# The fourth quarter of each middle head's exponentials goes through a transposing DMA, and values and the feed-forward halves change places

## The chip, the cores and the metric

One core of a Trainium2 chip runs the whole program in one launch. The metric is device time in microseconds: how long the one execution takes on the chip. The engines named below are TensorE (PE; its weight loads are listed as PEld), VectorE (DVE), ScalarE (ACT), GpSimd (POOL) and SyncE (SP), which here issues most of the DMAs.

## The reference

The program computes two layers on x (4 batches of 512 rows of 512). The first layer (a state space mixer and a mixture of experts) is not touched by the change. The second is cross-attention with 16 heads of 128 on a context of 512 rows, followed by a feed-forward block with ternary weights and 8-bit rows:

```python
    def _L1_xattn_ref(hidden_states, encoder_hidden_states, Wq, Wk, Wv, Wo, gq, gk):
        ...
        scale = 1.0 / np.sqrt(D)
        q = (hidden_states @ Wq).reshape(B, Sq, H, D)
        k = (encoder_hidden_states @ Wk).reshape(B, Skv, H, D)
        v = (encoder_hidden_states @ Wv).reshape(B, Skv, H, D)
        q = rmsnorm(q, gq)
        k = rmsnorm(k, gk)
        scores = jnp.einsum('bqhd,bkhd->bhqk', q, k) * scale
        attn = jax.nn.softmax(scores, axis=-1)
        out = jnp.einsum('bhqk,bkhd->bqhd', attn, v)
        out = out.reshape(B, Sq, H * D)
        return out @ Wo
    ...
        def bitlinear(x, w):
            xq = x + jax.lax.stop_gradient(activation_quant(x) - x)
            wq = w + jax.lax.stop_gradient(weight_quant(w) - w)
            return jnp.einsum('bsi,oi->bso', xq, wq)
        h = bitlinear(x, w1)
        h = jax.nn.gelu(h, approximate=False)
        return bitlinear(h, w2)
    ...
    x = x + _L1_xattn_ref(_layernorm(x, axis=-1), ctx_1024, ...)
    x = x + _L1_ffn_ref(_layernorm(x, axis=-1), L1_ffn_w1, L1_ffn_w2)
```

All values are 32-bit floats. What the change touches is the way from the scores to `attn` times `v`: the exponentials have queries on the partitions, and the product with `v` wants the context rows there, so each 128 x 512 block of weights must be transposed.

## The kernel before

The stage in question is the function `attend`. There are 64 heads over the batches, numbered n from 0 to 63 (16 a batch; groups of four heads share a load of `Wq` and `Wo`). Each head has four quarters i of 128 query rows. The main loop runs over units u = 4n + i, and the Python order in which instructions are written is the order in each engine's queue; every engine takes its queue in order.

In unit (n, i) are written, in this order:

- `scores(n, i)`: one PE matmul pair into `psc` (L1987; two such banks), DVE's row maximum `mx` (L1990), ACT's exponential `e` with its row sum (L1993).
- in unit i = 2, `values(n - 1)`: four PE matmuls (L2059, eight records in the trace) of `v` with `eT` of the head before, and ACT's copy of the result to `oT` (L2061). There is one `eT` buffer.
- what `front` holds for this unit: `project` (L2068, i = 0), `queries` (L1953, i = 1; ACT writes the squares `sq`, L1956), `turn_q` (L1980) and `turn_x` (L1907), and the feed-forward work on PE (`ffn_up` L2137, `ffn_hT` L2101, `ffn_down` L2172).
- `weights(n, i - 1)`: DVE divides `e` by its sum (L1998, L1999). Then `split` for that quarter, if it goes by DMA: ACT and POOL each copy one 16-bit half of the 32-bit numbers into `planes` (L2017, L2018; two buffers), and SP issues a transposing DMA from `planes` to `turned` (L2020; three buffers).
- `join` of a quarter whose transpose was issued two units ago: DVE and ACT copy the two halves from `turned` into `eT` (L2027, L2028).
- what `back` holds for this unit: the gathers of the expert rows (`fetch`, POOL L1874) and their sums (`add`, DVE L1882), loads (`load_q` L1917, `load_o` L1925, `load_kv` L1933 to L1939, all on SP), the norm of the queries, `scale_q` (DVE, `qn`, L1971), `split_q` and `join_q` (the same transposing DMA for the queries of three of four blocks), and the row work of the feed-forward block.

Which quarters go by DMA is told by `by_dma`: of heads 4 to 59 the first three; the fourth is transposed on PE by `turn` (four 128 x 128 transposes `pet`, L2052, and ACT's copy from PSUM to `eT`, L2053). In unit i = 1 `turn(n - 1, 3)` stands behind `queries`, and the join of the third quarter ahead of them; values of head n - 1 follow in unit i = 2:

```python
        if i == 2:
            values(n - 1)
        before, landed = divmod(u - 2, KB), divmod(u - 3, KB)
        behind = i == 1 and n < len(heads) - HG
        if not by_dma(*before) and not behind:
            turn(*before)
        if by_dma(*landed) and i == 1:
            join(*landed)
        do(front, u)
```

From batch 1 on, each group of four heads carries the feed-forward block of 128 rows of the batch before. Its up projection is done in two halves (`ffn_up`, with ACT's gelu), its hidden rows are rounded in quarters (`ffn_hq`: DVE, then POOL), transposed in halves (`ffn_hT`: the first on PE with a copy `Th` on ACT, L2102, the second by DMA), and the down projection is done in two halves. All four halves lie in units i = 3.

Of the kernel before, what the change touches and what calls it, by code (L numbers as in the profile page):

```python
# [17 lines left out]
F32 = mybir.dt.float32  # L18
# [3 lines left out]
I16 = mybir.dt.int16  # L22
# [8 lines left out]
P = 128  # L31
# [27 lines left out]
H, HD = 16, 128  # L59
HG = 4  # L60
# [1126 lines left out]
class Keys:  # L1187
# [4 lines left out]
    KB = S // P  # L1192
# [650 lines left out]
def attend(ctx, cm, x_all, w, kv, y_dram, wk, pos, tern, late, ctx_k, wk_k, out):  # L1843
# [6 lines left out]
    pool = {n: ctx.enter_context(tc.tile_pool(name=f"c_p{n}", bufs=n)) for n in (1, 2, 3, 4, 7)}  # L1850
# [6 lines left out]
    KB = S // P  # L1857
# [4 lines left out]
    heads = [(b, g, h) for b, g in groups for h in range(HG)]  # L1862
    xnTs, st = {}, {}
# [101 lines left out]
        nc.gpsimd.tensor_tensor(rq, ms, half, ALU.pow)  # L1965
        st[b, g]["q"] = pq, rq

    def scale_q(b, g):
        pq, rq = st[b, g]["q"]
        qn = st[b, g]["q"] = pool[1].tile([P, HG, HD], F32, name="qn")  # L1970
        nc.vector.tensor_tensor(qn, pq, rq.unsqueeze(2).to_broadcast([P, HG, HD]), ALU.mult)  # L1971

    def turn_q(b, g, i):
# [9 lines left out]
    def scores(n, i):  # L1983

        b, g, h = heads[n]
        pscore = psc.tile([P, S], F32, name="psc")
        nc.tensor.matmul(pscore, st[b, g]["qT"][:, h, i * P:(i + 1) * P], ks[n],  # L1987
                         start=True, stop=True)
        mx = small.tile([P, 1], F32, name="mx")
        nc.vector.tensor_reduce(mx, pscore, AX.X, ALU.max, negate=True)  # L1990
        e = pool[3].tile([P, S], F32, name="e")
        tot = small.tile([P, 1], F32, name="tot")
        nc.scalar.activation(e, pscore, AF.Exp, bias=mx, accum_out=tot)  # L1993
        es[n, i] = e, tot
# [5 lines left out]

    planes, turned = {}, {}

    def by_dma(n, i):
        if not HG <= n < len(heads) - 1:
            return False
        return i < (3 if n < len(heads) - HG else 2)

    def split(n, i):

# [3 lines left out]
    def turn_planes(e):  # L2013

        halves = e.bitcast(I16).rearrange("p (s two) -> p two s", two=2)
        t = pool[2].tile([P, 2, S], I16, name="planes")
        nc.scalar.copy(t[:, 1], halves[:, 1])  # L2017
        nc.gpsimd.tensor_copy(t[:, 0], halves[:, 0])  # L2018
        out = pool[3].tile([P, 2 * KB, P], I16, name="turned")
        nc.sync.dma_start_transpose(out, t.rearrange("p two s -> p (two s)"))  # L2020
        return out

    def join_planes(out, t, i):

        out = out.bitcast(I16).rearrange("p k (s two) -> p two k s", two=2)
        at = slice(i * P, (i + 1) * P)
        nc.vector.tensor_copy(out[:, 1, :, at], t[:, KB:])  # L2027
        nc.scalar.copy(out[:, 0, :, at], t[:, 0:KB])  # L2028

    def join(n, i):  # L2030

        if n not in eTs:
            eTs[n] = pool[1].tile([P, KB, S], F32, name="eT")
        join_planes(eTs[n][:, :, :], turned.pop((n, i)), i)
# [11 lines left out]
    def turn(n, i):  # L2046
        if n not in eTs:
            eTs[n] = pool[1].tile([P, KB, S], F32, name="eT")
        e, _ = es.pop((n, i))
        pt = ptr.tile([P, KB, P], F32, name="pet", tag="pt")  # L2050
        for kc in range(KB):
            nc.tensor.transpose(pt[:, kc, :], e[:, kc * P:(kc + 1) * P], cm.ident)  # L2052
        nc.scalar.copy(eTs[n][:, :, i * P:(i + 1) * P], pt)  # L2053

    def values(n):
        po = pav.tile([HD, S], F32, name="po")
        eT, v = eTs.pop(n), vs.pop(n)
        for kc in range(KB):
            nc.tensor.matmul(po, v[:, kc, :], eT[:, kc, :], start=kc == 0, stop=kc == KB - 1)  # L2059
        oTs[n] = pool[7].tile([HD, S], F32, name="oT")  # L2060
        nc.scalar.copy(oTs[n], po)  # L2061
# [124 lines left out]
    def put(where, u, f, *a):  # L2186
        where.setdefault(u, []).append((f, *a))

    last = len(groups) - 1
    for n, (b, g, h) in enumerate(heads):  # L2190
        j = n // HG
        u = n * KB
        if j < last and j > 0:
            after = groups[j + 1]
            put(front, u + 1, queries, *after, h)
            put(back, u + 2, norm_q, *after)
            put(back, u + 3, scale_q, *after)
            if h < HG - 1:
                put(back, u + 4, split_q, *after, h)
                put(back, u + 6, join_q, *after, h)  # L2200
        if j > 0:
            put(front, u + 4, project, j - 1, h)
        if j < last and j > 0 and h == HG - 1:
            put(front, u + 4, turn_q, *groups[j + 1], h)
        if j > 0:
            put(back, u + 5, take_projected, j - 1, h)
        if j > 0:
            put(back, u, load_q, j + 2, h, h + 1)
            put(back, u + 1, load_o, b, g, h, h + 1)
        put(back, u + 3, load_kv, n + 3)  # L2210
        put(back, u + 3, norm_k, n + 2)
        at = n % H
        if b + 1 < B:
            for k in range(3):
                if 0 <= 3 * (at - 2) + k < NC * TOPK:
                    put(back, u + k, add, 1)
            for k in range(3):
                if 0 <= 3 * (at - 1) + k < NC * TOPK:
                    put(back, u + (0, 1, 3)[k], fetch, 1)
            if at >= 11 and at < 15:  # L2220
                t = (b + 1) * NC + at - 11
                put(back, u + 1, stats, t, "c")
                put(back, u + 3, normed, t, "c")
                put(front, u + 4, turn_x, t)
        if b > 0 and h == 1:
            t = (b - 1) * NC + g
            put(back, u + 1, stats, t, "d")
            put(back, u + 3, ffn_x, t)
            put(back, u + 4, ffn_xq, t)
            put(front, u + 5, ffn_xT, t)  # L2230

            put(front, u + 7, ffn_up, t, 0)
            put(front, u + 11, ffn_up, t, 1)
            for k, at in enumerate((8, 9, 12, 12)):
                put(back, u + at, ffn_max, t, k)
            put(back, u + 12, ffn_h, t)
            for k in range(4):
                put(back, u + 13 + k // 2, ffn_hq, t, k)
            put(front, u + 14, ffn_hT, t, 0)
            put(front, u + 15, ffn_hT, t, 1)  # L2240
            put(front, u + 15, ffn_down, t, 0)
            put(front, u + 19, ffn_down, t, 1)
            put(back, u + 20, ffn_y, t)
            put(back, u + 20, store, t)

    def do(where, u):
        for f, *a in where.pop(u, []):
            f(*a)
# [24 lines left out]
    def later(time, f, *a):  # L2273
        steps.append((time, len(steps), f, a))
# [7 lines left out]
    for n in range(NC * TOPK):  # L2282
        at = n % 16 - KB
        if n >= 16 and 0 <= at < KB:
            at = -1
# [22 lines left out]
    for i in range(NC):  # L2308
        end = START + ((i + 1) * TOPK - 1) * GAP + FLIGHT
        later(end + 0.1, stats, i, "c")  # L2310
        later(end + 2.3, normed, i, "c")
        at = FRONT + i * WINDOW
        later(at, turn_x, i)
        later(at + 0.5, key_task)
        later(at + 2.2, queries, 0, 0, i)
        later(at + 5.6, key_ends)
        later(at + 6.4, norm_q, 0, 0)
        later(at + 6.5, queries, 0, 1, i)
        later(at + 8.5, scale_q, 0, 0)
        later(at + 10, turn_q, 0, 0, i)  # L2320
        later(at + 10.4, key_task)
        later(at + 10.8, norm_q, 0, 1)
        later(at + 12.1, scores, 0, i)
        later(at + 12.9, scale_q, 0, 1)
        later(at + 13, key_ends)
        later(at + 14, turn_q, 0, 1, i)
        if i < KB - 1:
            later(at + 14.7, weights, 0, i)
        if i < KB - 2:
            later(at + 15, turn, 0, i)  # L2330
# [30 lines left out]
    for u in range(KB, len(heads) * KB + 2):  # L2361
        n, i = divmod(u, KB)
        if n < len(heads):
            scores(n, i)
        if i == 2:
            values(n - 1)
        before, landed = divmod(u - 2, KB), divmod(u - 3, KB)
        behind = i == 1 and n < len(heads) - HG
        if not by_dma(*before) and not behind:
            turn(*before)  # L2370
        if by_dma(*landed) and i == 1:
            join(*landed)
        do(front, u)
        if not by_dma(*before) and behind:
            turn(*before)
        if n < len(heads):
            weights(*divmod(u - 1, KB))
            if by_dma(*divmod(u - 1, KB)):
                split(*divmod(u - 1, KB))
        if by_dma(*landed) and i != 1:  # L2380
            join(*landed)
        do(back, u)
        if u == len(heads) * KB:
            weights(*divmod(u - 1, KB))
# [159 lines left out]
```

## Time and profile before

| what | us |
|---|---|
| runs of the kernel before: median (lowest, highest) | 2475.75 (2473.74, 2478.19) |
| the profiled execution's own time | 2472.46 |
| its span | 2470.7 |
| mean granted TensorE clock | 0.979 |
| PE busy in the span | 2337.7 |
| values, L2059: busy, all heads | 236.8 |
| projection of queries, L1953 | 232.7 |
| scores, L1987 | 260.0 |
| output projection, L2068 | 231.2 |

The profile lists one execution. "Busy" is the time in which an engine had an instruction at work; for PE, whose matmuls are pipelined, the ends are modelled. The chain of waits follows the work that ended last back to what released it, so a piece on it is time that the span is made of. In a timeline the bracket behind an instruction tells how long its engine was idle before it, and what ended that. Each float matmul of 128 x 128 by 128 x 512 shows as two records. The attention stage with this loop lies at about 1390 to 2410 us of the span.

### The profile page before, as it was taken

The page shows a single profiled execution, that of the slowest core. Times are in us where ns is not written, and L with a number is a line of the kernel's source. Part 1 is how long each engine was busy: PE and PEld are TensorE (multiplying, and loading weights), DVE is VectorE, ACT ScalarE, POOL GpSimd, SP SyncE. Part 2 cuts the span into 40 slices and gives each one's busy share as a digit, 9 for nine tenths or more (in the row PEclk, how much of TensorE's full clock was granted, in tenths as well). Part 3 has the DMA queues.
Part 4 walks back from the last instruction along what each step waited for, and adds up shares of the span by engine and source line. Part 5 has one row for each costly group of instructions (what it writes and reads, how often), then busy time and mean ns, then how long its engine had stood idle before and what let it go on. Part 6 is the DMA issues. An engine that isn't in the chain of part 4 may idle for free. (4 is left out here: it accounts for less than half of the span.)

```text
span 2470.7 us, 29274 instructions
## 1 busy us (share of the span) xinstructions
PE 2337.7 (95%) x8915; PEld 1275.5 (52%) x8915; DVE 1595.2 (65%) x2848; ACT 1386.1 (56%) x2599; POOL 1344.1 (54%) x1323
## 2 busy tenths in 40 slices
PE   6989998988899999999998999999999999999998
PEld 2555555655556666666674444444444444444443
DVE  6999998966343444444324577667776777666655
ACT  6777777755333333342323466666666767667654
POOL 7999999950344455444434356356544665333323
PEclk8999999998999999999998999999999999999999
DMA  5252626343677777989866568778866887666530
GB/s 212 90 210 95 219 85 232 112 151 119 194 233 227 229 243 236 314 308 336 302 210 211 163 179 217 163 181 187 207 159 149 200 202 173 138 156 147 136 75 24
DMA packets 454245, 458.69 MB, mean 186 GB/s; under 512 B 289239, under 2 KB 330279, under 8 KB 449984
## 3 DMA queue, kind: packets, MB, share of 16 engines
q1 hardware_dynamic: 410622, 299.80, 43.4%
q0 software_dynamic: 41408, 156.76, 19.8%
q8 instruction: 73, 1.20, 0.2%
q14 instruction: 92, 0.75, 0.1%
q10 hardware_dynamic: 2050, 0.18, 0.1%
HBM read 312.74 MB, written 79.82 MB: 159 GB/s over the span
## 5 line engine op out<-in xcount | busy, mean ns | idle before, releaser
L1336 PE MATMUL pg<-xT,wg 128*128 128x284 f32 (+12 forms) x1536 | 392.7, 399 | 2.0 <-ACT xT L1303 1.1
L1990 DVE TENSOR_REDUCE mx<-psc 128x1 f32<-128x512 f32 x256 | 176.1, 688 | 244.4 <-PE psc L1987 244.0
L2018 POOL COPY planes<-e 128x512 int16<-128x512 int16 x174 | 119.1, 684 | 392.3 <-DVE e L1999 230.7
L1336 PEld LDWEIGHTS pg<-xT,wg 128*128 128x128 f32 x1536 | 277.8, 191 | 91.6 <-issue 40.9
L494 POOL TENSOR_TENSOR dBu<-bb,du 128x1024 f32<-128x1024 f32 x128 | 304.3, 2398 | 2.7 <-DVE dA L519 1.8
L1993 ACT ACTIVATE e<-psc,mx 128x512 f32<-128x512 f32 x256 | 176.3, 688 | 149.6 <-DVE mx L1990 81.8
L1987 PE MATMUL psc<-kT,qT 128*128 128x512 f32 x512 | 260.0, 594 | 0.0
L2059 PE MATMUL po<-eT,v 128*128 128x512 f32 x512 | 236.8, 605 | 10.4 <-ACT eT L2053 8.6
L1257 POOL DMA_INDIRECT xg<-xn_dram,tok x168 | 177.5, 1056 | 116.5 <-PE pt L1300 51.4
L1953 PE MATMUL pq<-Wq,xnT 128*128 128x512 f32 x512 | 232.7, 597 | 4.3 <-ACT xnT L1909 3.9
L2068 PE MATMUL px<-Wo,oT 128*128 128x512 f32 x512 | 231.2, 595 | 0.4 <-DVE qn L1971 0.4
L505 ACT ACTIVATE dA<-delta,negA 128x512 f32<-128x512 f32 x256 | 176.5, 695 | 52.1 <-DVE hc L520 29.1
L519 DVE TENSOR_TENSOR_SCAN dA<-dA,dBu 128x1024 f32<-128x1024 f32 x80 | 185.4, 2318 | 14.6 <-ACT dA L505 4.9
L1257 POOL DMA_INDIRECT wd<-down,widx x64 | 63.1, 986 | 237.9 <-PE po L1370 222.3
L2059 PEld LDWEIGHTS po<-eT,v 128*128 128x128 f32 x512 | 92.0, 189 | 147.5 <-issue 91.8
L1381 ACT COPY yo<-po 128x512 f32<-128x512 f32 (+3 forms) x64 | 37.5, 586 | 224.7 <-PE po L1370 185.3
L1953 PEld LDWEIGHTS pq<-Wq,xnT 128*128 128x128 f32 x512 | 96.5, 191 | 129.7 <-issue 110.4
L525 PEld LDWEIGHTS yT<-ident,hc 128*128 128x128 f32 x1024 | 119.5, 144 | 77.3 <-issue 40.5
L2068 PEld LDWEIGHTS px<-Wo,oT 128*128 128x128 f32 x512 | 95.1, 190 | 123.3 <-issue 102.8
L1874 POOL DMA_INDIRECT yg<-y_dram,pos x108 | 119.8, 1109 | 62.7 <-issue 50.4
L525 PE MATMUL yT<-ident,hc 128*128 128x128 f32 x1024 | 133.2, 278 | 19.8 <-DVE yg L559 9.2
L1381 DVE COPY yo<-po 128x512 f32<-128x512 f32 x68 | 46.9, 691 | 159.4 <-PE po L1370 159.4
(378 smaller groups left out, 4686.2 us busy)
## 6 DMA issues: line engine op xcount, KB each, us to landing
y_dram<-yo SPq DMA_DIRECT2D x110, 256.0 KB
bb<-bc_dram SPq DMA_DIRECT2D x16, 1024.0 KB
cb<-bc_dram SPq DMA_DIRECT2D x16, 1024.0 KB
v_dram<-v SPq DMA_DIRECT2D x64, 256.0 KB
k_dram<-k_kT SPq DMA_DIRECT2D x64, 256.0 KB
kT<-k_dram SPq DMA_DIRECT2D x64, 256.0 KB
rk<-r_dram SPq DMA_DIRECT2D x64, 256.0 KB
v<-v_dram SPq DMA_DIRECT2D x64, 256.0 KB
```

Of the source, the lines that this page charges most:

```text
L494: nc.gpsimd.tensor_tensor(dBus[q], st[b]["bb"][i // 2][:, j:j + 2, :], st[b]["du"][c].unsqueeze(1).to_broadcast([P, 2, S]), ALU.mult)
L505: nc.scalar.activation(dAs[q][:, j, :], st[b]["delta"][c], AF.Exp, scale=negA[:, c, n:n + 1])
L519: nc.vector.tensor_tensor_scan(*flat, 0.0, ALU.mult, ALU.add)
L525: nc.tensor.matmul(yT[:, lc, :], t[:, lc * P:(lc + 1) * P], cm.ident, is_transpose=True, start=first and lc == 0, stop=last, skip_group_ch ...
L1257: nc.gpsimd.indirect_dma_start(out=t[0:n, :], out_offset=None, in_=table, in_offset=bass.IndirectOffsetOnAxis(ap=index, axis=0))
L1336: nc.tensor.matmul(pg[:, 0:n], s["wg"][:, c, m * P:(m + 1) * P], s["xT"][:, c, 0:n], start=c == 0, stop=c == NC - 1)
L1953: nc.tensor.matmul(pq.rearrange("p h d -> p (h d)"), xnTs[b * NC + i][:, c, :], s["Wq"][:, c, :], start=c == 0, stop=c == NC - 1)
L1987: nc.tensor.matmul(pscore, st[b, g]["qT"][:, h, i * P:(i + 1) * P], ks[n], start=True, stop=True)
L1990: nc.vector.tensor_reduce(mx, pscore, AX.X, ALU.max, negate=True)
L1993: nc.scalar.activation(e, pscore, AF.Exp, bias=mx, accum_out=tot)
L2059: nc.tensor.matmul(po, v[:, kc, :], eT[:, kc, :], start=kc == 0, stop=kc == KB - 1)
L2068: nc.tensor.matmul(px, oTs[j * HG + h][:, i * P:(i + 1) * P], st[b, g]["Wo"][:, h, :], start=h == 0, stop=h == HG - 1)
```

## The change

`by_dma` says yes to all four quarters of heads 4 to 59 (`full`), so `turn` is left for the first four heads and the last four. For these heads `values(n - 1)` moves from unit i = 2 to i = 3, and the joins of head n - 1 lie in the units of head n: quarter 0 early in i = 0, quarter 1 late in i = 0, quarter 2 late in i = 1, quarter 3 early in i = 2. The feed-forward work of a group, without its first statistics, is put one unit earlier, so that its four halves fall into units i = 2. `turned` gets a fourth buffer, and `qn` takes the buffer of `sq` (in the first units, a `planes` buffer) instead of one of its own.

```diff
-    def scale_q(b, g):
+    def scale_q(b, g, into=(pool[1], "sq")):
         pq, rq = st[b, g]["q"]
-        qn = st[b, g]["q"] = pool[1].tile([P, HG, HD], F32, name="qn")
+        qn = st[b, g]["q"] = into[0].tile([P, HG, HD], F32, name="qn", tag=into[1])
         nc.vector.tensor_tensor(qn, pq, rq.unsqueeze(2).to_broadcast([P, HG, HD]), ALU.mult)
...
+    def full(n):
+        return HG <= n < len(heads) - HG
+
     def by_dma(n, i):
         if not HG <= n < len(heads) - 1:
             return False
-        return i < (3 if n < len(heads) - HG else 2)
+        return i < (KB if full(n) else 3 if n < len(heads) - HG else 2)
...
-        out = pool[3].tile([P, 2 * KB, P], I16, name="turned")
+        out = pool[4].tile([P, 2 * KB, P], I16, name="turned")
...
         if b > 0 and h == 1:
             t = (b - 1) * NC + g
             put(back, u + 1, stats, t, "d")
+            u -= full(n)
             put(back, u + 3, ffn_x, t)
...
-        later(at + 8.5, scale_q, 0, 0)
+        later(at + 8.5, scale_q, 0, 0, (pool[2], "planes"))
...
-        later(at + 12.9, scale_q, 0, 1)
+        later(at + 12.9, scale_q, 0, 1, (pool[2], "planes"))
...
-        if i == 2:
+        if i == (3 if full(n - 1) else 2):
             values(n - 1)
         before, landed = divmod(u - 2, KB), divmod(u - 3, KB)
         behind = i == 1 and n < len(heads) - HG
         if not by_dma(*before) and not behind:
             turn(*before)
-        if by_dma(*landed) and i == 1:
+        if full(n - 1) and i == 0:
+            join(n - 1, 0)
+        early = i == (2 if full(landed[0]) else 1)
+        if by_dma(*landed) and early:
             join(*landed)
         do(front, u)
...
-        if by_dma(*landed) and i != 1:
+        if by_dma(*landed) and not early and not (full(landed[0]) and i == 3):
             join(*landed)
         do(back, u)
```

## The prediction

> **What bounds the kernel now.** The page first, for the whole span: TensorE (PE) is the fullest engine.
>
> ```profile
> PE 2337.7 (95%) x8915; PEld 1275.5 (52%) x8915; DVE 1595.2 (65%) x2848; ACT 1386.1 (56%) x2599; POOL 1344.1 (54%) x1323
> ```
>
> The change touches only the attention stage (about 1390 to 2400 us of the span), so next the windows table, in three stretches of it: batch 0, which has no feed-forward work beside it; batches 1 and 2 with feed-forward and gathers of the expert rows; batch 3 with feed-forward and no gathers. After the time of a stretch come busy microseconds of PE, PEld, DVE, ACT, POOL, then clock, DMA share and GB/s.
>
> ```profile
> 1459.00:1546.00 87.00, 87.00 (x224) 39.05 (x223) 65.77 (x134) 56.60 (x116) 55.31 (x61) 1.00 0.88 217
> 1684.00:1784.00 100.00, 98.38 (x286) 44.03 (x286) 79.65 (x168) 64.37 (x123) 63.98 (x74) 1.00 0.84 195
> 2170.00:2301.00 131.00, 130.54 (x377) 58.34 (x376) 86.04 (x196) 90.11 (x169) 48.03 (x69) 1.00 0.65 147
> ```
>
> PE is busy 98 to 100% everywhere; ACT is at 65 to 69%, DVE at 66 to 80%, and the 16 DMA engines are at 0.84 to 0.88 wherever rows are gathered. So PE work taken out counts in full, as long as nothing on PE has to wait for what replaces it. The chain of waits for one head of batch 0 (start, us, what) shows the order on PE:
>
> ```profile
> 1511.61 0.86 PE psc L1987 x2
> 1512.47 3.43 PE pq L1953 x8
> 1515.90 0.44 PE pet L2052 x4
> 1516.34 0.86 PE psc L1987 x2
> 1517.20 3.57 PE po L2059 x8
> 1520.77 1.72 PE psc L1987 x4
> 1522.48 3.43 PE px L2068 x8
> ```
>
> The chain never leaves PE here. What is to be seen is how values (po) are kept from waiting: the fourth quarter is transposed at 1515.90 (pet), and ACT has the 1.30 us of pet and scores (psc) to copy it out. ACT's timeline shows that it just makes it:
>
> ```profile
> 1515.94 0.60 ACT L1956 ACTIVATE sq<-pq 128x512 f32<-128x512 f32 x1 [0.66 <-PE pq L1953]
> 1516.43 0.58 ACT L2053 COPY eT<-pet 128x512 f32<-128x512 f32 x1
> 1516.90 0.63 ACT L2017 COPY planes<-e 128x512 int16<-128x512 int16 x1
> 1517.96 0.69 ACT L1993 ACTIVATE e<-psc,mx 128x512 f32<-128x512 f32 x1 [0.43 <-DVE mx L1990]
> ...
> 1525.27 0.76 ACT L2028 COPY eT<-turned 128x512 int16<-128x512 int16 x1
> 1525.89 0.61 ACT L2017 COPY planes<-qn 128x512 int16<-128x512 int16 x1
> ...
> 1527.62 0.69 ACT L1993 ACTIVATE e<-psc,mx 128x512 f32<-128x512 f32 x1 [1.12 <-DVE mx L1990]
> ...
> 1528.30 0.76 ACT L2028 COPY eT<-turned 128x512 int16<-128x512 int16 x1
> ```
>
> The eT copy ends at 1517.01, 1.11 us after the queries (pq) ended. Last, the chain of waits in batches 1 and 2:
>
> ```profile
> 1701.42 6.54 DMA turned<-planes
> ...
> 1718.17 0.04 issue
> 1718.22 3.70 PE po L2059 x8
> ...
> 1755.06 1.03 ACT Th L2102
> 1756.08 0.05 issue
> 1756.13 1.90 PE pf L2172 x8
> ```
>
> A transposing DMA that took 6.54 us held DVE up, then ACT, and in the end values at 1718.22 (the timeline gives PE 1.16 us of idle time there). At 1756.13 the down projection waits for ACT's copy of the hidden rows (0.23 us of idle PE, 11 times).
>
> **The change part by part.** Write (n, i) for quarter i of head n; head n's four steps also carry the joins and values of head n-1.
>
> (a) Removed: pet of 56 heads (4 to 59). 56 x 0.44 = 24.6 us of PE, all on the chain. One ACT copy of 0.58 each goes too.
>
> (b) Added per head: ACT planes 0.62 and join 0.77, DVE join 0.45, POOL planes 0.68, an SP issue of 1.24, and 256 KB through the DMA engines. The trace has 24,087 packets of 256 bytes in the first stretch, 35.4 us of 16 engines; at 1,024 a transpose, 1.5 us each. Per head of 16 us all this is 5% of ACT, 3% of DVE, 4% of POOL, 9% of DMA; none becomes full, though DMA comes to 0.95 where rows are gathered. As shares these cost nothing; PE covers them. What counts is their place in the queues: (d) and (e).
>
> (c) The feed-forward halves come one step earlier, and values one step later (third to fourth step). The first half of Th is now copied under queries (3.43) instead of under scores (0.86), so the 0.23 us waits go: 11 x 0.23 = 2.5. Three old waits of values for a copy of eT fall with that copy, at 1651.34, 1718.22 and 2348.98: 0.93 + 1.16 + 1.79 = 3.9.
>
> (d) What values wait for now: ACT's join of (n-1,3). In ACT's order after queries stand sq, planes of (n,0), join of (n-1,2), exp of (n,2), join of (n-1,3). From start to start in the rows above: 0.04 + 0.49 + 0.51 (planes to the next start, 1523.15 to 1523.66 in the trace) + 0.62 + 0.68, then 0.76 for the join and 0.06 until PE starts (as at 1718.22): 3.16 us after queries end. PE meanwhile has scores, the feed-forward half if there is one, scores: 0.86 + 1.73 + 0.86 = 3.45, so 0.29 to spare. Without a half it has only 1.72. The halves reach the third step of heads 18 to 60 but not of heads 5 to 17. There values start 1.44 late, and the eight matmuls run 0.13 longer after a wait (3.70 against 3.57): 13 x 1.57 = 20.4 us. This is the term I trust most, since it needs nothing but ACT's order.
>
> (e) The landing of (n-1,3). Count from the end of the previous values (0), when scores of (n,0) start. ACT does oT, then planes of (n-1,2), to 1.1; SP issues that transpose (1.24), the three loads of load_kv (0.52, 0.43, 0.55 and gaps), then (n-1,3) at about 4.1; two gelus in the step before (two table loads of 1.28 and 1.27 of gelu) push this to 5.4. From issue to the last semaphore update, transposes issued just after load_kv took 3.05 to 8.68 us, median 4.6; 6.1 to 6.8 in batch 0, 5.9 on the mean with gathers and feed-forward, 4.1 without gathers, 4.7 on every other one. ACT needs 2.63 after the landing (planes of (n,0) has to wait for the same planes buffer, of which there are two). Late beyond (d) then: batch 0, 4.1 + 6.1 = 10.2 against 9.1, 1.1 in 6 gathering heads, 6.6 in all; with gathers, 0.7 + 0.7 + 2.0 for a group of four heads, 5.25 groups, 18; without, 0.7 a group, 5.5 groups, 4. Behind ACT's waiting join stand gelu, the planes of (n,1) and the next exp; behind DVE's the weights of (n,1). Bounds 0 and 29. The old rows had other gathers beside them (two just before, one of them now later), so I take the middle, 14.
>
> (f) hT of the first half now stands on PE one step after hq, and not after values; behind it queue queries. By the rows POOL ends hq about 0.5 us before; the wait of DVE for a landing in that place (1.63 at 1748.60) would make it 1.1 late. In 5.25 groups: 0 to 6, I take 3. Behind values and hT on PE stands everything else; nothing of PE passes them.
>
> (g) qn in the buffer of sq: the next sq comes a step after planes of qn on ACT and POOL, 3 us later by the rows; 0, covered by scores and queries, and 0.6 (one copy) a head if POOL were that late. The fourth turned buffer, and the planes buffers used by the first four heads' qn: 0, at most 1 either way.
>
> [...]
>
> [...] Here 256 KB took 1.5 us of the engines, some 175 GB/s. [...]
>
> Sum: -24.6 - 2.5 - 3.9 + 20.4 + 14 + 3 = +6.4 us. The profiled execution took 2472.46 (span 2470.7 and 1.8 around it), so 2478.9; it lies 3.3 below the median of the runs, 2475.75, so there 2482.
>
> **The rivals.**
> Landings in time: (e) and (f) are 0, only batch 0 pays. -10.6, 2465. For it: only one landing in five groups held PE up by over 1 us before. Against: then they had a step more cover, or nobody needed them at once.
> PE stays the bound everywhere (faster): values never wait, because sq or planes overlap more than the rows show. -31, 2445. It needs the 1.44 of (d) to vanish; against it is that ACT takes its queue in order in every row.
> The DMA queue takes over (slower): DMA at 0.95 and six transposes in flight make landings longer than 6 us, (e) at its upper bound or above, with (f): 6.4 + 15 + 3 = +24, 2500. It decides from a landing 5 us after the issue on. For it: 8.68 at 1695.59 and 6.4 to 6.7 at five places under gathers.
>
> **How the numbers follow.** About 0.2% (5 us) is what a measurement can tell from no change. Forecast 0.50 (2482, its own range 2472 to 2492); landings in time 0.16; PE bound 0.09; DMA queue 0.25. Faster: 0.09 + 0.15 + 0.02 = 0.26. Same: 0.16 from the forecast's lower part. Slower: 0.58. The range takes in the first and last rival: 2460 to 2508.
>
> **What would show it.** In batch 0 the period from values to values goes from 14.3 to about 15.5, with PE idle 1.4 before po and ACT's eT join as releaser: (d). If it stays under 14.1, (d) is wrong. In batch 3 a group of four heads goes from 65.6 to about 64.3. PE idle before pth would show (f); joins released by the landing, in the chain of waits, (e). What would make me wrong most: landings that get shorter since transposes and gathers meet less often, or DVE, at 80%, reaching the maxima late.

## The result, and the profile after

| | median us | runs, lowest to highest | profiled execution's span |
|---|---|---|---|
| kernel before | 2477.63 | 2473.74 to 2485.09 | 2470.7 |
| changed kernel | 2545.63 | 2536.06 to 2552.42 | 2543.4 |

The changed kernel is slower: ratio 1.0259, 95% interval 1.0242 to 1.0277, some 68 us in the medians and 72.7 us between the two profiled spans. Of these 72.7 us, 66.5 lie between the first and the last values of the attention stage (998.9 us before, 1065.4 after); 6.2 lie ahead of it, where the traces differ without regard to the change: the first values start at 1409.7 us before and 1416.0 after, and in the variants below, most of which have the same beginning, at 1408.8 to 1430.7. Below, `po` stands for the first matmul of values, and lines of the changed file are 3 higher than before (values L2062, ACT's and POOL's planes copies L2020 and L2021, the joins L2030 and L2031).

The page of the changed kernel, first its busy times and then the chain that ended last:

```profile
PE 2337.8 (92%) x8691; PEld 1261.4 (50%) x8691; DVE 1622.9 (64%) x2904; ACT 1423.5 (56%) x2655; POOL 1377.3 (54%) x1379
...
PE 19%; DMA 11%; DVE 7%; ACT 6%; issue 2%; POOL 2%; SPq 1%; POOLq 0%; DVEq 0%; ACTq 0%
```

Two things are to be seen. PE is busy for as long as before, 2337.8 against 2337.7 us, though 224 matmul instructions are gone: its work must have become slower somewhere (in the stage itself, 974.4 against 979.5 us). And the chain, 37% of the span on PE before, is now 19% on PE and 11% on DMAs.

The windows table of the changed kernel, for a stretch of batch 0, one of 15 us in batch 2, and one of batch 3 (columns as in the prediction):

```profile
1459.00:1546.00 87.00, 76.28 (x169) 32.53 (x168) 58.70 (x119) 51.95 (x105) 48.95 (x57) 0.94 0.89 200
1965.00:1980.00 15.00, 10.36 (x22) 4.41 (x23) 6.24 (x13) 9.45 (x15) 7.01 (x8) 0.77 0.76 133
2199.00:2332.00 133.00, 127.48 (x346) 55.61 (x345) 88.34 (x204) 95.70 (x177) 54.11 (x76) 1.00 0.77 164
```

PE is no longer full in any of them, and the clock column, 1.00 in the three stretches shown before, drops to 0.94 and 0.77 in the first two. Who ended the waits in the attention stage (us in total, times, longest):

```profile
POOL planes L2021 <- DMA turned<-planes: 235.1, 89, 9.1
...
ACT planes L2020 <- DMA turned<-planes: 76.0, 48, 8.6
...
PE po L2062 <- ACT eT L2031: 63.7, 41, 4.5
...
PE ph L2140 <- DMA Tx<-xq: 9.8, 8, 3.4
...
PE pth L2104 <- POOL hq L1835: 5.9, 7, 2.0
```

Values wait 63.7 us for ACT's join. ACT's planes copies wait 76.0 us for the landing of an earlier transpose (0.6 us before the change), POOL's 235.1. The two last lines, for the transposed feed-forward rows (Tx) and for the rounded hidden rows (hq), are waits that the kernel before did not have. POOL's line before the change (1400 to 2400 us) was:

```profile
POOL planes L2018 <- DMA turned<-planes: 39.0, 27, 3.7
```

How a wait in batch 0 comes about, from the chain of waits of the changed kernel:

```profile
1613.32 3.53 PE pq L1953 x8
...
1616.95 0.10 ACT sq L1956
...
1617.44 0.61 ACT planes L2020
1618.05 0.43 ACT eT L2031
1618.48 0.10 issue
1618.58 0.77 ACT e L1993 x2
1619.35 0.67 ACT eT L2031
1620.02 0.04 issue
1620.06 3.70 PE po L2062 x8
```

Queries end at 1616.85, values start 3.21 us later, behind ACT's row of five (sq, planes, join, exp, join). The worst wait with feed-forward work, in batch 2, from SP's timeline, ACT's timeline and the chain:

```profile
1957.49 0.44 SPq L1933 DMA_DIRECT2D kT<-k_dram  x1
...
1959.16 1.31 SPq L2100 DMA_TRANSPOSE Tx<-xq  x1
1960.58 3.14 SPq L2023 DMA_TRANSPOSE turned<-planes  x1
```

```profile
1962.86 0.60 ACT L1956 ACTIVATE sq<-pq 128x512 f32<-128x512 f32 x1 [1.66 <-PE pq L1953]
1969.78 0.62 ACT L2020 COPY planes<-e 128x512 int16<-128x512 int16 x1 [6.32 <-DMA turned<-planes]
```

```profile
1960.58 9.13 DMA turned<-planes
...
1969.73 0.46 DVE eT L2030
...
1971.70 0.66 ACT eT L2031
1972.36 0.04 issue
1972.40 2.93 PE po L2062 x3
```

The fourth quarter's transpose is issued behind three loads and the transpose of the feed-forward rows, and lands after 9.13 us. ACT stands for 6.32 us at the next planes copy, since both planes buffers are in flight; when it goes on, it is the row that the prediction put at 2.63 us (1969.71 to 1972.40) to values. PE was idle for 4.47 us.

### The profile page after: what moved, and what is told of

It is laid out like the page before. It is cut to its first block, busy times and chain, and to the rows that moved or that the text cites. A ratio compares the mean times of both kernels' runs of the same rounds, so it can differ in the third digit from the quotient of the medians.

```text
span 2543.4 us, 29312 instructions
## 1 busy us (share of the span) xinstructions
PE 2337.8 (92%) x8691; PEld 1261.4 (50%) x8691; DVE 1622.9 (64%) x2904; ACT 1423.5 (56%) x2655; POOL 1377.3 (54%) x1379
## 3 DMA queue, kind: packets, MB, share of 16 engines
q0 software_dynamic: 41408, 156.76, 20.6%
## 5 line engine op out<-in xcount | busy, mean ns | idle before, releaser
L2021 POOL COPY planes<-e 128x512 int16<-128x512 int16 x230 | 154.0, 670 | 406.5 <-DMA turned<-planes 181.1
L2062 PE MATMUL po<-eT,v 128*128 128x512 f32 x512 | 249.6, 633 | 71.5 <-ACT eT L2031 64.8
L2062 PEld LDWEIGHTS po<-eT,v 128*128 128x128 f32 x512 | 96.9, 199 | 222.4 <-ACT eT L2031 109.8
L2031 ACT COPY eT<-turned 128x512 int16<-128x512 int16 x230 | 175.3, 762 | 4.1 <-DMA turned<-planes 4.1
L2020 ACT COPY planes<-e 128x512 int16<-128x512 int16 x230 | 142.1, 618 | 59.2 <-DMA turned<-planes 56.3
L1381 ACT COPY yo<-po 128x512 f32<-128x512 f32 (+3 forms) x64 | 37.5, 585 | 230.5 <-PE po L1370 189.9
```

## The experiments

All of them change the changed kernel. In the table, columns 3 to 7 come from each run's trace: idle time of PE before po of heads 4 to 16 and of heads 17 to 59, before the up projection for Tx, before pth for hq, and time in the attention stage with the granted clock at 0.5. Ratios are to the kernel before on the same chip; its median was 2477.63 to 2487.91 us on the chips used, so medians of different runs are best compared by their ratios.

| run | ratio, 95% interval | po 4-16 | po 17-59 | Tx | hq | half clock |
|---|---|---|---|---|---|---|
| kernel before | | 0 | 3.9 | 0 | 0 | 0 |
| changed | 1.0259 (1.0242 to 1.0277) | 23.4 | 41.5 | 9.9 | 5.9 | 37.5 |
| planes3 | 1.0206 (1.0172 to 1.0240) | 22.5 | 19.9 | 14.0 | 10.6 | 27.3 |
| kv_later | 1.0128 (1.0092 to 1.0163) | 22.5 | 14.7 | 0.3 | 16.2 | 20.5 |
| from17 | 1.0189 (1.0152 to 1.0226) | 0 | 40.7 | 14.8 | 2.6 | 41.0 |
| halves_back | 1.0341 (1.0303 to 1.0378) | 25.1 | 71.3 | 0.2 | 2.7 | 44.4 |
| planes3_kv | 0.9945 (0.9920 to 0.9971) | 19.6 | 1.1 | 0 | 3.4 | 3.4 |
| join_first | 0.9901 (0.9870 to 0.9931) | 10.8 | 0 | 0 | 6.6 | 0 |
| joins_early | 0.9865 (0.9838 to 0.9891) | 3.6 | 0 | 0 | 6.6 | 0 |
| joins_early17 | 0.9883 (0.9848 to 0.9918) | 0 | 0.7 | 0 | 6.2 | 3.4 |
| order_only | 1.0131 (1.0103 to 1.0160) | 15.9 | 20.6 | 15.6 | 10.0 | 30.7 |
| late45 | 1.0033 (1.0016 to 1.0051) | 0 | 1.3 | 12.9 | 0 | 3.4 |
| late45_loads | 0.9953 (0.9935 to 0.9970) | 0 | 4.1 | 0 | 0 | 0 |

**planes3**: a third planes buffer.

```diff
-        t = pool[2].tile([P, 2, S], I16, name="planes")
+        t = pool[3].tile([P, 2, S], I16, name="planes")
```

(and the two other users of that tag.)

> The changed kernel with three planes buffers instead of two, nothing else. Theory A (a fourth transpose in the first step makes the planes copies of (n,0) wait for the landing of (n-1,3), and sq, planes, join and exp stand in a row behind that landing on ACT before values may start): after the landing ACT then needs 0.8 us instead of 2.6, so the 41 us that values wait in heads 18 to 60 fall to 5 to 15, the half-clock stretches (37 us of them in the changed kernel) to under 10, and the time to about 2495 (2480 to 2510). The 13 heads of batch 0 keep 1.4 to 1.5 us each. Rival B (the DMA engines are full, so it is landings as such): the same time as the changed kernel, 2535 to 2550. Rival C (the halves one unit earlier are what costs: waits for Tx and hq): no change either, those waits stay at 16 us.

Measured 2529.78 us. POOL's wait for landings fell from 235 to 3.5 us and values of heads 17 to 59 wait half as long, but 19.9 us were left, the clock still dropped, and Tx and hq waited longer. So two buffers are half of that wait, and the time expected was too good. What is left is the landing itself, for which ACT's joins now wait (3.4 us in the changed kernel):

```profile
ACT eT L2031 <- DMA turned<-planes: 38.1, 18, 5.5
```

**kv_later**: three loads a head go one unit later, behind the transposes.

```diff
-        put(back, u + 3, load_kv, n + 3)
+        put(back, u + 4, load_kv, n + 3)
```

> The changed kernel with the three loads of load_kv issued one unit later, behind the transposes of (n-1,3) and of the queries instead of ahead of them. Theory A with the landing as its late part: (n-1,3) is issued 0.5 to 1 us earlier and lands after about 3.3 instead of 4.8 us, so waits of values in heads 18 to 60 fall from 41 to 10 to 20 us, half-clock stretches to under 15 us, time about 2505 (2490 to 2520). Rival B (DMA engines full whatever the order): 2535 to 2550. The batch 0 waits stay at 1.4 to 1.5 us a head.

Measured 2509.71 us, as theory A has it, though 20.5 us at half clock are left where under 15 were expected. The same DMAs in another order save 36 us, so it is not that the DMA engines are full. In heads 18 to 59 the fourth quarter's transpose now lands 3.25 us after its issue, where it took 4.9 in the changed kernel (medians, to the last semaphore update). Tx, no longer behind those loads, made PE wait 0.3 us.

**from17**: four quarters by DMA only where a feed-forward half stands between queries and values.

```diff
-        return HG <= n < len(heads) - HG
+        return H < n < len(heads) - HG
```

> The changed kernel with four quarters by DMA for heads 17 to 59 only; heads 4 to 16 are as before the change. Theory A: the 23 us that values wait in batch 0 go, and the half-clock stretches there (14 us, worth 7), and 13 transposes on PE come back (6 us): 24 us less than the changed kernel, 2521 (2514 to 2528). If batch 0 cost only what its waits show without the clock, 2528. Rival B (DMA engines full): batch 0 has no slower DMA than before in its landings, so about 2540.

Measured 2525.80 us, 20 less than the changed kernel: batch 0 alone costs that much. In the traces heads 4 to 17 took 216.0 us, 234.0 in the changed kernel and 206.3 before. The half clock did not fall in all (41.0 us against 37.5): more of it came in the later heads.

**halves_back**: the feed-forward work returns to its old units.

```diff
-            u -= full(n)
```

> The changed kernel with the feed-forward work at its old units (halves in the fourth step, beside values). Theory A: no head has more than 1.7 us of PE work between queries and values, so values of heads 18 to 60 wait 1.4 us or more each as in batch 0; waits for Tx (10 us) and hq (6 us) go, the waits of values grow by 35 to 60 us: 2570 to 2600. Rival C (the earlier halves are what costs): 2525 to 2535.

Measured 2562.24 us, a little less than expected: values wait 30 us more, Tx and hq 13 less. The earlier halves are cover, and on balance not the cost.

**planes3_kv**: both edits, of planes3 and of kv_later, together.

> The changed kernel with both: three planes buffers, and the loads of load_kv one unit later. Theory A (the landing of (n-1,3) and the planes buffers behind it are two parts of one wait): waits of values in heads 17 to 59, 20 us with the third buffer and 15 with the later loads, fall to 3 to 10; half-clock stretches from 20 to about 12 us; time 2498 (2490 to 2505). Rival (either of them takes away all that can be had, and what is left is DMA traffic under the gathers): 2505 to 2512. Batch 0 keeps 22 us and hq some 16 us in both.

Measured 2473.84 us against 2485.66 of the kernel before beside it: faster than before the change, and far better than expected. Apart the two edits took 0.5 and 1.3% off the ratio (16 and 36 us), together 3.1%. The chain of this run, in batch 3, never leaves PE:

```profile
2250.97 3.43 PE pq L1953 x8
2254.40 0.86 PE psc L1987 x2
2255.26 1.73 PE ph L2140 x8
2256.99 0.86 PE psc L1987 x2
2257.85 3.50 PE po L2062 x8
```

and the stage's waits show that planes copies hardly wait for a landing any more (3.1 us where POOL had 235.1), and that values wait in batch 0:

```profile
PE po L2062 <- ACT eT L2031: 20.7, 15, 1.5
...
POOL planes L2021 <- DMA turned<-planes: 3.1, 4, 1.5
```

**join_first**: on top of that, the join of (n-1,3) is written ahead of scores (n,2).

```diff
+        early = i == (2 if full(divmod(u - 3, KB)[0]) else 1)
+        ahead = early and full(n - 1)
+        if ahead:
+            join(*divmod(u - 3, KB))
         if n < len(heads):
             scores(n, i)
...
-        early = i == (2 if full(landed[0]) else 1)
-        if by_dma(*landed) and early:
+        if by_dma(*landed) and early and not ahead:
             join(*landed)
```

> As planes3_kv, and the join of (n-1,3) stands ahead of scores (n,2) in the program, so that ACT does it before the exp of (n,2) and not behind it. Theory A (in batch 0 values wait for ACT's row of sq, planes, join, exp, join after queries): without exp the row is 2.5 us and not 3.2, so values of heads 4 to 16 wait 0.75 us each, 10 us in all in place of 22, and the time is some 12 us below planes3_kv. Rival (batch 0 waits for a landing): the 22 us stay, or grow since DVE then waits for the landing ahead of the maxima.

Measured 2459.35 us. 13 waits of 0.83 on the mean instead of 1.5: taking exp out of ACT's row takes 0.68 off, as its rows say.

**joins_early**: on top of join_first, the join of (n-1,2) also goes ahead, in front of queries.

```diff
+        early = early or i == 1
         if by_dma(*landed) and early and not ahead:
             join(*landed)
```

> As join_first, and the join of (n-1,2) stands ahead of queries instead of behind sq and the planes copy. Theory A: behind queries ACT then has sq, planes and one join, 1.9 us against 1.7 of PE, so values of heads 4 to 16 wait 0.1 to 0.3 us in place of 0.83 (10.8 us before, now under 5), and the time is 6 to 9 us below join_first: ratio to the kernel before about 0.987. Rival (the landing of (n-1,2) is late at that place and holds DVE and ACT): no gain over join_first, waits in heads 17 to 59 come back.

Measured 2452.04 us, ratio 0.9865: the fastest version, 1.3% below the kernel before. Its windows table:

```profile
1684.00:1784.00 100.00, 97.43 (x267) 43.67 (x268) 84.99 (x181) 69.43 (x132) 70.53 (x81) 1.00 0.96 217
2170.00:2301.00 131.00, 131.00 (x363) 58.84 (x362) 90.95 (x214) 99.65 (x185) 54.23 (x80) 1.00 0.78 171
```

The DMA share is 0.96 under the gathers, higher than in the changed kernel (0.87 in the same stretch), and PE is busy for 97.43 of the 100 us all the same; values wait nowhere in heads 17 to 59.

**joins_early17**: joins_early with the range of from17.

> As joins_early, with four quarters by DMA only from head 17 on. Theory A: once values no longer wait in batch 0, the 13 heads gain by the DMA as well, so leaving them out costs their transposes on PE, 13 x 0.44 = 6 us, less what they still wait: 3 to 6 us above joins_early. Rival (batch 0 is better off with its transposes on PE): below joins_early.

Measured 2463.58 us, 11.5 above joins_early where 3 to 6 were expected; its interval overlaps that of joins_early, and one of its four runs took 2448.89. The two traces speak for theory A: heads 4 to 17 took 210.0 us here and 205.6 in joins_early, and the stage 973.9 against 968.8, while 12.8 us more passed here ahead of the stage. That is one trace each, so the size stays open.

**order_only**: the two joins moved as in joins_early, with two planes buffers and the loads where they were.

> The changed kernel with the two joins moved as in joins_early, but with two planes buffers and the loads where the change has them. Theory A in two parts: the waits of batch 0 go (23 us to under 8), but the planes copies still wait for landings, so values of heads 17 to 59 wait 25 to 40 us, Tx 10, and half-clock stretches stay at 20 to 35 us: 2510 to 2525. Rival (the order on ACT alone is the cause): 2455 to 2465, as with all three.

Measured 2520.94 us. The order on ACT alone takes the ratio from 1.0259 to 1.0131, half of the loss; the rest stays with the landings. The two parts were split differently than expected: 15.9 us of waits in batch 0 (under 8 expected), 20.6 behind it (25 to 40).

**late45**: planes3_kv with all four quarters by DMA for heads 45 to 59 alone.

```diff
-        return HG <= n < len(heads) - HG
+        return 45 <= n < len(heads) - HG
```

> As planes3_kv, with four quarters by DMA for heads 45 to 59 alone, where a feed-forward half stands between queries and values and no rows are gathered. Heads 44 to 60 took 261.0 us in the kernel before and 249.6 us in planes3 and 248.8 in kv_later. Theory A: nothing waits there, 15 x 0.44 of PE, four waits for Th of 0.23 and one wait of values of 1.79 go, 9 us together: the time is 9 to 11 us below the kernel before, ratio 0.996. Rival (the gain there is eaten by the step from one order to the other, or shows as a later wait at the end): within 3 us of the kernel before.

Measured 2494.71 us: slower, a miss. Heads 44 to 60 gained (250.1 against 261.0 us), but heads 17 to 44, which keep the old order, took 467.0 instead of 451.4. Their chain says why:

```profile
1793.92 0.55 SPq L1939
...
1794.51 0.62 SPq L1917
...
1795.23 6.53 DMA Tx<-xq
```

In the old order the later loads come right ahead of the transpose of the feed-forward rows, and the up projection waits 12.9 us for it in all.

**late45_loads**: late45 with load_kv back in its place.

```diff
-        put(back, u + 4, load_kv, n + 3)
+        put(back, u + 3, load_kv, n + 3)
```

> As late45, but load_kv stays where the change and the kernel before have it. Theory (the 9 us that late45 lost are the loads of load_kv put right ahead of the transposing DMA of xq in heads 17 to 44, which keep the order of before: 12.9 us of PE waiting for Tx): those waits go, heads 17 to 44 take 451 us as in the kernel before (467 in late45), heads 44 to 60 some 250 against 261: 8 to 11 us below the kernel before, ratio 0.996. Rival (the third planes buffer, or the step from one order to the other, is what costs): as late45, 1.003.

Measured 2470.25 us, ratio 0.9953: as expected, waits for Tx are 0, heads 17 to 44 take 453.5 us, heads 44 to 60 250.9. The last two runs also tell that joins_early's gain in heads 17 to 44 (435.6 us, 451.4 before) does not come from the third planes buffer or the later loads by themselves: with the fourth quarter on PE the buffer left 453.5 us, and the loads with it 467.0.

## Why the prediction was wrong

It forecast slower, and why, but 6.4 us where 72.7 came. The step that failed is (e), the landing of the fourth quarter, mis-sized by 31 us; and the fall of the clock was not in the sum at all. By its steps, in the profiled executions:

- (a) The transposes of PE went: 24.6 us (24.2 of them in the stage, counted from its first to its last values). The chain of planes3_kv in batch 3, without a pet in it, agrees.
- (d) ACT's row between queries and values held to 0.05 us: 3.21 against 3.16 in the head shown, and 3.18 to 3.33 in nine of the thirteen heads. Values waited 23.4 us in batch 0 where 18.7 were forecast (20.4 with the restart); 13 x 1.5 = 19.5 of it are the row, and the rest are late landings in four heads. join_first and joins_early take it apart piece by piece.
- (e) failed in its size. The step let one landing be late, from a fixed issue at 4.1 or 5.4 us after the values before, and took half of what the old rows gave: 14 us, at most 29. Measured: 41.5 us in heads 17 to 59 and some 4 in batch 0, 31 more than the sum had. In heads 18 to 59 the landings were about as long as counted, 4.9 us in the median (the step had 4.1 to 5.9), with single ones up to 9.77. It was the issue that came later. Told by the place of the head in its group of four, medians in us after the values before: 4.5 in the first head (4.1 counted), 6.2 in the third and fourth, which follow gelus (5.4 counted), and 6.4, up to 8.1, in the second, where SP sends Tx ahead of it, which the step did not count at all (4.1 counted). In the first to fourth heads values wait 3.7, 20.2, 13.5 and 4.1 of the 41.5 us. What takes the wait away is shown: kv_later makes the landing shorter (3.25 us), with planes3 no planes copy on ACT waits for a landing any more, and planes3_kv, with both, brings 41.5 to 1.1, while each alone leaves 15 to 20. It is tempting to say that the wait feeds itself, a late landing holding the next planes copy and so the next issue; that is argued and not shown, for with planes3 alone the issue comes no earlier (6.2 us in the median of heads 18 to 59, as in the changed kernel).
- (c) The waits of 0.23 for Th went (one of 1.2 near the end came), but the step saw no price in the earlier halves. The up projection now comes after queries and not after values, and waited 9.9 us for Tx. halves_back and kv_later each bring that wait down to 0.2 or 0.3.
- (f) was 5.9 us where 3 was taken, within its bounds.
- (g) cost nothing that shows.
- Not in the sum at all: the clock. PE was granted half its clock for 37.5 us, and was busy in 33.8 of them; if that work took twice as long as at full clock, as the eight matmuls below did (5.98 us for 3.03), it is 33.8 / 2 = 16.9 us. With a remainder of 2.2 us, which no run takes apart, this is what PE's busy time in the stage failed to fall by: it fell by 5.1 us where the transposes alone were 24.2. It is worked out from the trace, not shown by a run that changes the clock alone.

So in the stage -24.2 + 61.1 (waits of values, all heads) + 9.9 + 5.9 + 16.9 + 2.2 - 4.2 (queries' waits for xnT, gone) - 1.1 for small ones = 66.5, which is what the stage grew by; the other 6.2 of the 72.7 lie ahead of it.

Of the rivals, "the DMA queue takes over" was nearest, with the right place and a third of its price. Its reason, engines at 0.95, was wrong: joins_early runs at 0.96 in a stretch where no values wait, and in kv_later the same transposes land in 3.25 us. "Landings in time" is what planes3_kv made true; its 10.6 us of gain were 12 in the medians.

With buffers and order mended the DMA's way is the faster one here, 1.3% below the kernel before (joins_early, ratio 0.9865), where PE, busy for 95% of the span before, is the full engine. It is not the shorter way: the four transposes of a quarter took PE 0.44 us, and the transposing DMAs of the changed kernel took 3.03 to 9.77 us from issue to landing.

## What to carry to other kernels

Where a full engine's work is handed to DMAs, count how many are in flight at once against the buffers in front of them: a copy that waits for a buffer stands, with all behind it on its engine, until a transfer has landed (6.32 us on ACT, up to 1969.78, in the changed kernel). Read the order on the issuing queue, and count all that is sent ahead of the transfer that somebody waits for: the same loads one place later were worth 36 us here, and in the other order (late45 against late45_loads) cost 13.5 us over heads 17 to 44. And a chain that ends just in time on one engine (1.11 of 1.30 us before) must be recounted when its last link moves.

## What the runs showed of the hardware

TensorE's clock fell to half for 3.41 or 6.83 us at nine places of the changed kernel's attention stage, 37.5 us in all. In the kernel before it stayed at 1.00 in the stage, where PE was never idle for more than 1.79 us at a time. The first drop, from PE's timeline:

```profile
1469.42 6.65 PE L2062 MATMUL po<-eT,v 128*128 128x512 f32 x8 [3.24 <-ACT eT L2031]
```

The eight matmuls took 6.65 us, where the eight at 1620.06 took 3.70. The drop lasted from 1468.57 to 1475.40, so 5.98 of the 6.65 us lie in it and 0.67 behind it; at full clock what was done in those 5.98 us would take 3.70 - 0.67 = 3.03 (worked out from these rows).

In the changed kernel's stage PE was idle for over 2 us at a time at twelve places. Nine of these idle times (2.03 to 4.47 us) were followed by a drop, each drop after 2.03 to 3.19 us of idle PE in the 3.41 us ahead of it; three were not (2.47 us up to 1504.47, 2.03 up to 1773.99, 2.12 up to 1793.00). In length the two kinds overlap; in place they differ. The nine drops start whole multiples of the shortest, 3.41 us, apart (the nearest two 6.83 us, 1826.97 and 1833.80). With the stage divided at that spacing, the nine stretches at full clock in which PE was idle for 2.03 us or more are those that half clock followed, and none with 1.96 us or less was followed by it; each of the three idle times without a drop lies across two stretches. That is one trace, and no run moves a wait alone, so that the place decides is not shown.
